# Layer 1 of the last two graphs regrouped, and unread TensorE products at both ends, in a two-layer graph-attention kernel

## The chip, the cores and the metric

The kernel runs on one core of a Trainium2 chip. The metric is the device time of one execution in microseconds (us). The core has five engines, each with an instruction queue of its own that is worked off in order: TensorE (PE in the profile, with its weight loads as PEld), VectorE (DVE), ScalarE (ACT), GpSimd (POOL) and SyncE (SP). DMA transfers are issued from POOL's and SP's queues.

## The reference: what is computed

The input x has 32 graphs of 512 nodes with 512 features, and all graphs share one 512 x 512 adjacency with about four neighbours to a node. Everything is float32. Both layers are added to x behind a layer norm and a relu (cut to its core):

```python
h = max(layernorm(x), 0)                              # layer 0: attention, 8 heads of 64
q, k, v = h @ Wq + bq, h @ Wk + bk, h @ Wv + bv
attn = softmax(q k^T / 8 + (1 - adj) * -1e9)
x = x + (attn @ v) @ Wo + bo
h = max(layernorm(x), 0)                              # layer 1: additive attention
g = h @ W
e = leaky_relu(g @ a1 [:, None] + g @ a2 [None, :], 0.2) * adj
x = x + elu(softmax(e) @ g + beta * g)
```

In layer 1 an edge that is absent has the score 0, not minus infinity, so every node also takes part in the sum of all nodes.

## The kernel before, in words

**Tiles.** A graph is four tiles of 128 nodes. The prediction numbers the token tiles of the second stage n = 4b + t with b the stage (0 to 33) and t the tile. The weights stay in SBUF. The neighbours of a tile's nodes are listed as edges; 128 edges make a group, and a tile has NG = 4 groups. Rows of keys, values and the layer-1 state are stored in DRAM tables (`tab`, for the last two stages `th`) and gathered back edge by edge by an indirect DMA from POOL, one for each group.

**Stages.** `stage_a(b)` makes q, k and v of graph b and stores them. `stage_b(b)` does layer 0 of graph b and, LAG = 2 graphs behind, layer 1 of graph b - 2. For b = 32 and 33 there is no layer 0 left (`s is None`): these two stages, n = 128 to 135, are layer 1 of the last two graphs, 30 and 31.

**One layer-1 tile** has these steps: four gathers (L946), the edge weights z (L1127 to L1134: sum of two scores, leaky relu on DVE, exponent on ACT, minus 1 on DVE), the weights spread to a one-hot matrix `wv` (L1140, DVE), the edge sums on PE (L987, four groups), a product that adds the denominators when there is no layer 0 (line 42 from `layer1`), the denominators on DVE (L1162 to L1164), the node's own row relu(norm(x1)) on ACT (L756) and its addition on DVE (L1170), four transposes on PE (L737), the addition of the column sums `cs` on ACT in four instructions (L1181), the product with W on PE (line 42 from `dense`, four blocks, eight records in the trace), two evictions on ACT (L1190, L1191), two elu steps on DVE (L1195, L1196) and a keep, the indirect DMA that writes the tile out (L767, POOL).

**What layer 1 needs of a whole graph.** The column sums `cs` and, in the last two graphs, s1: `spread_s1` transposes it on PE (L1100), writes it as one row to DRAM and reads it back to all partitions (SP, L1103 and L1108), and DVE picks the entries of each edge (L1112, L1113). A gather needs all four tiles of the graph stored (L1067).

**What sets the order.** Nothing is scheduled by hand. Each step is recorded with `op(engine, us, key, ...)`, with a cost and a due time `key`; S = 20 is the due-time distance of two tiles. `Plan.order` walks through time with these costs and picks, engine by engine, the ready operation with the lowest key. Its buffers are rings: `kv` (5 buffers of 128 x 2 x 1552, two to a tile), `oT` and `gT` (1 each, the transposed tiles), `w` (4), `z` (4), `wv` (2), six PSUM buffers `D` and one, `X`. A buffer is free when its last reader is done. The order found is fixed in the program; changing a key or a ring moves instructions of every queue.

**Start.** `setup` fills constants on DVE and POOL; x of graph 0 is loaded first, then the adjacency and the weights in pieces from SP (L775, L377, L645). The first PE work is `turned_state`'s transposes of the normed tiles, then `edges`' product for the node ranks (its input from L421) and the products with Wq, Wk and Wv.

Of the kernel before, what the change touches and what calls it, by code (L numbers as in the profile page):

```python
# [218 lines left out]
def kernel(  # L219
# [49 lines left out]
    def ring(n, shape, name):  # L269
# [52 lines left out]
    oh = OH.rearrange("p (g r) -> p g r", r=G)  # L322

    C_ = {n: buf(None, n) for n in (
        "wq", "wk", "wv", "wo", "w1", "rows", "c_row", "wa", "OH", "nzE", "idx", "qidx", "fin",
# [3 lines left out]
    def setup():  # L329
        nc.gpsimd.iota(OH.bitcast(I32), pattern=[[1, D]], base=1, channel_multiplier=0)  # L330
        nc.gpsimd.iota(idx[:, 0, 0:1], pattern=[[1, 1]], base=0, channel_multiplier=1)
        make_identity(nc, ident)
        nc.gpsimd.memset(mhalf, -0.5)
        nc.vector.memset(rings["qe"][-1], 0.0)
        nc.vector.memset(one32, 1.0 / G)
        for b in rings["hx"]:
            nc.vector.memset(b[:, D:], 0.0)
        for b in rings["q"]:
            nc.vector.memset(b[:, D:], 0.0)
        for b in rings["v"]:  # L340
# [343 lines left out]

    KD = 110.0

    def dot_rows():
# [47 lines left out]
    def turned(p, src):  # L735
        for c in range(C):
            nc.tensor.transpose(p[:, ts(c, P)], src[:, ts(c, P)], ident)  # L737
# [32 lines left out]
    def turned_state(b, t, key, mv):  # L770
        xb = buf("x", f"x{b}_{t}")
        if b:
            op("POOL", 1.3, key - 2.0 * S, lambda: fetch(xb.ap, b, t), r=[C_["perm"]], w=[xb], dma=P * D * 4)
        else:
            op("SP", 0.1, -90.0 + 0.01 * t, lambda: nc.sync.dma_start(xb.ap, x[0, ts(t, P), :]), w=[xb], dma=P * D * 4)  # L775
        norm(key - 1.3 * S, xb, mv, t, f"a{b}_{t}")
        op("ACT", 0.8, key - 0.9 * S, lambda: relu(xb.ap, xb.ap, mv.ap, t), r=[(mv, t)], w=[xb])
        pt, hT = buf("D", "pt"), buf("hT", f"hT{b}_{t}")
        kt = key + ((0.48, -0.51)[t % 2] if b else -0.51) * S
        o = op("PE", 0.45, kt, lambda: turned(pt.ap, xb.ap), r=[xb], w=[pt])  # L780
        plan.reserve(o, hT)
        op("ACT", 0.6, kt, lambda: nc.scalar.copy(hT.ap.rearrange("p c q -> p (c q)"), pt.ap), r=[pt], w=[hT])  # L782
        return hT
# [150 lines left out]
    def stage_b(b):  # L934
# [16 lines left out]
        for t in range(T):  # L951
            kb = base(T * b + t)
            slots = [buf("kv", f"kv{b}_{t}_{i}") for i in range(2)]
            held = [{n: buf(None, n) for n in ("K", "V", "H")} for _ in range(2)]
            of = {KO: "KVH", VO: "VH", HO: "H"}
            for g in range(NG):
                for tab, c0, c1 in st[b]["tab"]:
                    op("POOL", 1.3, kb - 0.85 * S + 0.1 * g, lambda sl=slots[g // 2], g=g, t=t, tab=tab, c0=c0, c1=c1: gather(
                        sl.ap[:, g % 2, c0:c1], tab, t, g),
                       r=[tab, C_["idx"]],  # L960
                       w=[(slots[g // 2], (g % 2, c0)), *((held[g // 2][n], (g % 2, "row")) for n in of[c0])],
                       dma=P * (c1 - c0) * 4)
# [18 lines left out]
        if s is not None:  # L981
            self_sums(b, base(T * b + 6))

    def edge_sums(out, lhs, slots, c0, n):

        for g in range(NG):
            nc.tensor.matmul(out(g), lhs(g), slots[g // 2].ap[:, g % 2, c0 : c0 + n], start=True, stop=True)  # L987

# [3 lines left out]
    def layer0(b, t, kb, slots, held, qs, weights):  # L992
# [126 lines left out]
    def edge_weights(b, t, kb, slots, held, qs):  # L1119

        s = st[b]
        k1 = kb + 0.6 * S
        z, wvb = buf("z", f"z{b}_{t}"), buf("wv", f"wv{b}_{t}")
        for i in range(2):
            def add(i=i):
                s1 = s["s1e"].ap[:, t, 2 * i : 2 * i + 2] if qs is None else qs[i].ap[:, :, D]
                nc.vector.tensor_tensor(z.ap[:, 2 * i : 2 * i + 2], s1, slots[i].ap[:, :, HO], op=ALU.add)  # L1127

# [7 lines left out]
        if b + LAG < B:  # L1136
            for i in range(2):
                op("DVE", 0.1, k1, lambda i=i: nc.vector.tensor_copy(
                    slots[i].ap[:, :, HO], z.ap[:, 2 * i : 2 * i + 2]), r=[z, (slots[i], "use")], w=[(held[i]["H"], "z")])
        op("DVE", 0.35, k1, lambda: nc.vector.tensor_tensor(  # L1140
# [4 lines left out]
    def layer1(b, t, kb, slots, held, wvb, pv):  # L1145
        s = st[b]
        px, g = buf("D", f"pg{b}_{t}"), buf("w", f"g{b}_{t}")
        o = op("PE", 1.02, kb + S, lambda: edge_sums(
            lambda i: px.ap[ts(i, G), :], lambda i: wvb.ap[:, ts(i, G)], slots, HO + 1, D),
               r=[*((x, "use") for x in slots), *((h["H"], "rows") for h in held), wvb], w=[px], form=4)  # L1150
        plan.reserve(o, g)
        k = kb + S
        x1, dn = s["x1"][t], s["dn"]
        op("ACT", 0.8, k, lambda: relu(g.ap, x1.ap, s["mv1"].ap, t), r=[x1, (s["mv1"], t)], w=[g])

        if pv is None:
            pd = buf("D", f"pn{b}_{t}")
            op("PE", 0.2, kb + S, lambda: product(nc, pd.ap[:, 0:1], wvb.ap, one32[:, 0:1]), r=[wvb], w=[pd])

# [24 lines left out]

        op("ACT", 1.5, k + 0.485 * S, add_all, r=[pt, s["cs"]], w=[gT])
        oo = op("PE", 3.43, k + 0.88 * S, lambda: dense(py.ap, gT.ap, w1), r=[gT, C_["w1"]], w=[py])
        plan.reserve(oo, y)
# [9 lines left out]

        op("ACT", 1.36, k + 1.05 * S, halves, r=[(dn, t)], w=[py, y])
        op("DVE", 1.45, k + 1.05 * S, elu, r=[py, x1], w=[y])
        op("POOL", 1.3, k + 1.2 * S, lambda: keep(y.ap, b, t), r=[y, C_["perm"]], dma=P * D * 4)  # L1200

# [247 lines left out]
```

## Time and profile before

| | us |
|---|---|
| median of 3 runs | 2736.29 (2734.39 to 2737.78) |
| profiled execution | 2723.47 |
| its span, first to last instruction | 2721.6 |
| PE busy | 2648.3 (97%) |
| DVE busy | 2049.9 (75%) |
| ACT busy | 1934.4 (71%) |
| POOL busy | 1831.2 (67%) |
| last W product on PE ends | 2711.4 |

The page is of one execution. A line of a timeline gives the start and the length in us, engine, source line, operation, output and input names with their shapes, a count, and in brackets the idle time of the engine just before and what ended it ("<-DVE w L1038": DVE's write of w at line 1038). "issue" is idle time for which the profile shows no other engine. A stretch's line gives its length and each engine's busy time with the number of its instructions, then the granted clock, the DMA share and GB/s. A product of float32 128 x 128 with 128 x 512 shows as two records; at the full clock records follow each other at 0.43 us, at half the clock at 0.85 us.

### The profile page before, as it was taken

The numbers are of one execution on the slowest core, as the hardware profiler recorded it, in microseconds if no ns is written. First come the engines' busy times: TensorE is split into PE (matmuls) and PEld (weight loads), VectorE is DVE, ScalarE is ACT, GpSimd is POOL, SyncE is SP. The second block draws the span as 40 slices with busy tenths as digits, with TensorE's granted clock in tenths as the row PEclk, the third lists the DMA queues.
The fourth block names the chain that finished last, engine by engine and source line by source line (L and its number), as shares of the span: only waits on it lengthen the run. The fifth ranks groups of instructions, "written<-read, shape, count | busy, mean of one in ns | idle before, by whom it ended". The sixth has DMA issues, their size and how long they took to land.

```text
span 2721.6 us, 39762 instructions
## 1 busy us (share of the span) xinstructions
PE 2648.3 (97%) x10220; PEld 1213.2 (45%) x10220; DVE 2049.9 (75%) x5200; ACT 1934.4 (71%) x6215; POOL 1831.2 (67%) x1710
## 2 busy tenths in 40 slices
PE   8999999999999999999999999999999999999886
PEld 4444444444444444444444444444444444444332
DVE  7768777777777777777777777777777777777663
ACT  1557777687877777777777777777777777777763
POOL 2776766666766766766766776676676676675763
PEclk9999999999999999999999999999999999999988
DMA  5988998888988988988988988988888888888863
GB/s 180 252 290 320 307 307 291 297 294 305 311 296 289 321 292 296 314 297 288 316 298 292 326 291 290 321 289 303 312 296 292 305 309 303 297 310 286 303 211 117
DMA packets 237457, 790.08 MB, mean 290 GB/s; under 512 B 34667, under 2 KB 34675, under 8 KB 237222
## 3 DMA queue, kind: packets, MB, share of 16 engines
q0 software_dynamic: 156736, 644.99, 70.3%
q1 hardware_dynamic: 80486, 142.48, 14.0%
q8 instruction: 83, 1.36, 0.2%
q14 instruction: 152, 1.25, 0.1%
HBM read 617.88 MB, written 169.46 MB: 289 GB/s over the span
## 4 chain that ended last, share of the span: by engine, by line
PE 88%; DMA 3%; issue 3%; DVE 2%; ACT 2%; POOL 2%; POOLq 0%; SPq 0%; DVEq 0%; ACTq 0%
PE pd L42 46%; PE pd L858 26%; PE pd L737 6%; PE pd L987 4%; PE px L987 4%; DMA qe<-qtab,qidx 1%; ACT kv L1014 1%; PE pd L918 1%; DMA kv<-tkv,idx 1%; PE pd L1081 1%; POOL kv L946 1%; POOL qe L968 0%; POOL x L762 0%; DMA x<-in_x_dram,perm 0%; DVE s L1003 0%
## 5 line engine op out<-in xcount | busy, mean ns | idle before, releaser
L1014 ACT ACTIVATE kv<-kv 128x64 f32<-128x64 f32 x4096 | 1011.8, 335 | 5.2
L968 POOL DMA_INDIRECT qe<-qtab,qidx x512 | 556.0, 1086 | 223.0 <-issue 114.0
L946 POOL DMA_INDIRECT kv<-tab,idx x480 | 508.2, 1059 | 164.6 <-issue 113.6
L42 PE MATMUL pd<-wo,oT 128*128 128x512 f32 x1032 | 468.6, 597 | 2.5 <-ACT oT L1051 2.4
L42 PE MATMUL pd<-w,gT 128*128 128x512 f32 x1024 | 466.1, 598 | 3.6 <-ACT gT L1181 3.6
L42 PE MATMUL pd<-wq,hT 128*128 128x512 f32 x1024 | 465.0, 597 | 2.2 <-ACT hT L782 2.2
L762 POOL DMA_INDIRECT x<-in_x_dram,perm x252 | 359.5, 1426 | 85.1 <-issue 50.3
L1000 DVE TENSOR_TENSOR qe<-qe,kv 128x1024 f32<-128x1024 f32 x256 | 312.1, 1220 | 44.4 <-DMA qe<-qtab,qidx 35.6
L1003 DVE TENSOR_REDUCE s<-qe 128x16 f32<-128x1024 f32 x256 | 310.5, 1214 | 0.1
L42 PEld LDWEIGHTS pd<-w,gT 128*128 128x128 f32 x1024 | 195.7, 192 | 249.5 <-issue 234.0
L42 PEld LDWEIGHTS pd<-wo,oT 128*128 128x128 f32 x1032 | 196.3, 192 | 245.0 <-issue 222.0
L42 PEld LDWEIGHTS pd<-wq,hT 128*128 128x128 f32 x1024 | 195.4, 192 | 245.6 <-issue 241.7
L749 POOL TENSOR_TENSOR mv<-mv,mhalf 128x1 f32<-128x1 f32 x256 | 171.4, 670 | 177.5 <-DVE mv L746 156.7
L767 POOL DMA_INDIRECT out_dram<-w,perm x128 | 157.3, 1229 | 149.8 <-DVE w L1196 105.7
L858 PE MATMUL pd<-wk,hT 128*128 128x512 f32 x496 | 239.7, 607 | 3.7 <-ACT hT L782 3.4
L858 PE MATMUL pd<-wt,S 128*128 128x512 f32 x496 | 238.5, 603 | 4.5 <-DVE k L866 4.1
L858 PE MATMUL pd<-wv,S 128*128 128x512 f32 x496 | 233.6, 593 | 3.1 <-DVE v L866 1.8
L1190 ACT ACTIVATE w<-pd,dn 128x512 f32<-128x512 f32 x128 | 87.6, 684 | 185.8 <-PE pd L42 185.5
L1061 DVE CUSTOM_DVE_ANT_0 w<-hx,wa_r 128x512 f32<-128x512 f32 x256 | 175.1, 684 | 11.3 <-ACT hx L756 10.5
L1053 DVE TENSOR_TENSOR x<-pd,x 128x512 f32<-128x512 f32 x128 | 87.9, 687 | 121.8 <-PE pd L42 110.1
L744 DVE BATCH_NORM_STATS2 st<-x 128x6 f32<-128x512 f32 x256 | 176.3, 689 | 3.8 <-DMA x<-in_x_dram 1.0
L737 PE MATMUL pd<-ident,w 128*128 128x128 f32 x1152 | 154.3, 276 | 21.7 <-DVE w L1038 11.2
(204 smaller groups left out, 3504.7 us busy)
## 6 DMA issues: line engine op xcount, KB each, us to landing
qtab<-q SPq DMA_DIRECT2D x124, 258.0 KB
tab<-hx SPq DMA_DIRECT2D x120, 260.0 KB
tab<-v SPq DMA_DIRECT2D x120, 260.0 KB
tab<-k SPq DMA_DIRECT2D x120, 256.0 KB
qe<-qtab,qidx POOLq DMA_INDIRECT x512, 7.8
kv<-tab,idx POOLq DMA_INDIRECT x480, 8.0
x<-in_x_dram,perm POOLq DMA_INDIRECT x252, 8.0
th<-hx SPq DMA_DIRECT2D x8, 260.0 KB
```

What stands on the lines that cost most here:

```text
L42: nc.tensor.matmul(out, lhsT, rhs, start=start, stop=stop)
L737: nc.tensor.transpose(p[:, ts(c, P)], src[:, ts(c, P)], ident)
L744: nc.vector.bn_stats(s6.ap, src.ap)
L762: nc.gpsimd.indirect_dma_start(dst, None, rows, bass.IndirectOffsetOnAxis(ap=perm[:, t : t + 1], axis=0), **lim)
L858: nc.tensor.matmul(p.ap, lhs()[:, c, :], rhs[:, c, :], start=first and c == 0, stop=c == K2 - 1, skip_group_check=True)
L946: nc.gpsimd.indirect_dma_start(dst, None, tab.ap, bass.IndirectOffsetOnAxis(ap=idx[:, t, g : g + 1], axis=0), bounds_check=N + DUMMY - 1, ...
L968: op("POOL", 1.3, kb - 0.84 * S + 0.1 * g, lambda q=qs[g // 2], g=g, t=t: nc.gpsimd.indirect_dma_start(q.ap[:, g % 2, :], None, s["qtab"]. ...
L987: nc.tensor.matmul(out(g), lhs(g), slots[g // 2].ap[:, g % 2, c0 : c0 + n], start=True, stop=True)
L1000: nc.vector.tensor_tensor(qe.ap[:, :, 0:D], qe.ap[:, :, 0:D], sl.ap[:, :, KO : KO + D], op=ALU.mult)
L1003: nc.vector.tensor_reduce(sb.ap, qe.ap[:, :, 0:D].rearrange("p n (h f) -> p n h f", f=HD), axis=AX.X, op=ALU.add)
L1014: nc.scalar.activation(p[:, h, 0:HD], p[:, h, 0:HD], AF.Copy, scale=p[:, h, HD : HD + 1])
L1061: nc.vector.tensor_tensor_reduce(scr.ap, hx.ap[:, 1 : D + 1], row, 1.0, 0.0, op0=ALU.mult, op1=ALU.add, accum_out=dst)
```

## The change

Layer 1 of the last two stages (b + LAG >= B in `layer1`, `s is None` in `stage_b`) is regrouped, and some products are added whose result nobody reads.

- **Rows in one buffer.** A tile of the last two stages takes one `kv` buffer and not two; its four rows of 520 lie one after the other in it. `row` and `weights_of` give the addresses of both layouts.
- **Sums ahead of products.** The due times of a layer-1 tile in the last two stages are moved: weights at 0.2 S after its base and not 0.6 S, edge sums at 0.5 S and not 1.0 S, while transposes, W product and evictions keep near the old ones. So the recorded order puts the edge sums of a tile ahead of the W product of the tile before.
- **One add.** The four additions of `cs` on ACT become one instruction on DVE, and the transposed tile lies in `gT` and `oT` in turn.
- **Unread products.** `run_on` records a number of 128 x 128 by 128 x 512 products into a PSUM buffer that is written again before it is read. At the start three of them, on a constant block that DVE sets to 1 (`first`), ahead of the first transposes. Near the end three each at n = 124 and 125, which wait for the tile's first gather, and one each for n = 123 to 127, behind the edge sums of layer 0. In PE's order the two threes come to lie just ahead of Wo of n = 122 and between the two transposes of n = 123.

PE's order is the same as before from the first transposes until n = 122, and so is that of the other queues up to there, DVE's new memset aside.

```diff
@@ setup
+        nc.vector.memset(first[:, 0:D], 1.0)
@@
+    GL, ZL = 0.5, 0.2
...
+    def run_on(key, n, bank, src, us=0.86, behind=()):
+
+        def prod():
+            for _ in range(n):
+                product(nc, bank.ap, src[:, 0:P], src[:, 0:D])
+
+        op("PE", us * n, key, prod, r=behind, w=[bank])
@@ turned_state
+        if b == 0 and t == 0:
+            run_on(kt, 3, pt, first, 1.7)
@@ stage_b
-            slots = [buf("kv", f"kv{b}_{t}_{i}") for i in range(2)]
+            slots = [buf("kv", f"kv{b}_{t}_{i}") for i in range(2 if s is not None else 1)]
+            slots += slots[len(slots) - 1 :] * (2 - len(slots))
@@
+    def row(slots, g, c0, n):
+
+        if slots[0] is slots[1]:
+            return slots[0].ap.rearrange("p a b -> p (a b)")[:, g * HW_ + c0 - HO : g * HW_ + c0 - HO + n]
+        return slots[g // 2].ap[:, g % 2, c0 : c0 + n]
@@ layer0
+        if T * b + t > T * (B - 1) - 2:
+            run_on(k + 0.01, 1, pt, wq[:, 0, :], behind=[px])
@@ edge_weights
-        k1 = kb + 0.6 * S
+        k1 = kb + (0.6 if b + LAG < B else ZL) * S
@@ layer1
-        o = op("PE", 1.02, kb + S, lambda: edge_sums(
+        last = b + LAG >= B
+        k = kb + (GL if last else 1.0) * S
+        kt, kw, ke = (0.6 - GL, 1.7 - GL, 1.75 - GL) if last else (0.485, 0.88, 1.05)
+        if b + LAG == B - 1 and t < 2:
+            run_on(k - 0.2, 3, px, wq[:, 0, :], behind=[(slots[0], (0, KO))])
+        o = op("PE", 1.02, k, lambda: edge_sums(
...
-        pt, gT, py, y = buf("D", "pt"), buf("gT", f"gT{b}_{t}"), buf("D", "py"), buf("w", f"y{b}_{t}")
-        oo = op("PE", 0.45, k + 0.485 * S, lambda: turned(pt.ap, g.ap), r=[g], w=[pt])
+        pt, gT, py, y = buf("D", "pt"), buf("oT" if last and t % 2 else "gT", f"gT{b}_{t}"), buf("D", "py"), buf("w", f"y{b}_{t}")
+        oo = op("PE", 0.45, k + kt * S, lambda: turned(pt.ap, g.ap), r=[g], w=[pt])
...
+        def add_at_once():
+            nc.vector.tensor_tensor(
+                gT.ap, pt.ap.rearrange("p (c q) -> p c q", c=C), s["cs"].ap.unsqueeze(2).to_broadcast([P, C, P]), op=ALU.add)
+
+        if last:
+            op("DVE", 0.72, k + kt * S, add_at_once, r=[pt, s["cs"]], w=[gT])
+        else:
+            op("ACT", 1.5, k + kt * S, add_all, r=[pt, s["cs"]], w=[gT])
+        oo = op("PE", 3.43, k + kw * S, lambda: dense(py.ap, gT.ap, w1), r=[gT, C_["w1"]], w=[py])
```

More of the change, by code (lines that the diff above doesn't have):

```diff
@@ L322 @@
     oh = OH.rearrange("p (g r) -> p g r", r=G)
+    first = rings["kv"][0][:, 0, :]
     C_ = {n: buf(None, n) for n in (
@@ L957, in stage_b @@
                 for tab, c0, c1 in st[b]["tab"]:
-                    op("POOL", 1.3, kb - 0.85 * S + 0.1 * g, lambda sl=slots[g // 2], g=g, t=t, tab=tab, c0=c0, c1=c1: gather(
-                        sl.ap[:, g % 2, c0:c1], tab, t, g),
+                    op("POOL", 1.3, kb - 0.85 * S + 0.1 * g, lambda slots=slots, g=g, t=t, tab=tab, c0=c0, c1=c1: gather(
+                        row(slots, g, c0, c1 - c0), tab, t, g),
                        r=[tab, C_["idx"]],
-                       w=[(slots[g // 2], (g % 2, c0)), *((held[g // 2][n], (g % 2, "row")) for n in of[c0])],
+                       w=[(slots[g // 2], (g, c0)), *((held[g // 2][n], (g % 2, "row")) for n in of[c0])],
                        dma=P * (c1 - c0) * 4)
@@ L982, in stage_b, with weights_of @@
             self_sums(b, base(T * b + 6))
+    def row(slots, g, c0, n):
+        if slots[0] is slots[1]:
+            return slots[0].ap.rearrange("p a b -> p (a b)")[:, g * HW_ + c0 - HO : g * HW_ + c0 - HO + n]
+        return slots[g // 2].ap[:, g % 2, c0 : c0 + n]
+    def weights_of(slots, i):
+        if slots[0] is slots[1]:
+            flat = slots[0].ap.rearrange("p a b -> p (a b)")[:, 0 : NG * HW_]
+            return flat.rearrange("p (g c) -> p g c", g=NG)[:, 2 * i : 2 * i + 2, 0]
+        return slots[i].ap[:, :, HO]
     def edge_sums(out, lhs, slots, c0, n):
         for g in range(NG):
-            nc.tensor.matmul(out(g), lhs(g), slots[g // 2].ap[:, g % 2, c0 : c0 + n], start=True, stop=True)
+            nc.tensor.matmul(out(g), lhs(g), row(slots, g, c0, n), start=True, stop=True)
     def use(slots, held, names):
@@ L1126, in add @@
                 s1 = s["s1e"].ap[:, t, 2 * i : 2 * i + 2] if qs is None else qs[i].ap[:, :, D]
-                nc.vector.tensor_tensor(z.ap[:, 2 * i : 2 * i + 2], s1, slots[i].ap[:, :, HO], op=ALU.add)
+                nc.vector.tensor_tensor(z.ap[:, 2 * i : 2 * i + 2], s1, weights_of(slots, i), op=ALU.add)
             op("DVE", 0.2, k1, add, r=[*([s["s1e"]] if qs is None else [(qs[i], "use"), qs[i].s1]),
@@ L1138, in edge_weights @@
                 op("DVE", 0.1, k1, lambda i=i: nc.vector.tensor_copy(
-                    slots[i].ap[:, :, HO], z.ap[:, 2 * i : 2 * i + 2]), r=[z, (slots[i], "use")], w=[(held[i]["H"], "z")])
+                    weights_of(slots, i), z.ap[:, 2 * i : 2 * i + 2]), r=[z, (slots[i], "use")], w=[(held[i]["H"], "z")])
         op("DVE", 0.35, k1, lambda: nc.vector.tensor_tensor(
@@ L1151, in layer1 @@
         plan.reserve(o, g)
-        k = kb + S
         x1, dn = s["x1"][t], s["dn"]
@@ L1157, in layer1 @@
             pd = buf("D", f"pn{b}_{t}")
-            op("PE", 0.2, kb + S, lambda: product(nc, pd.ap[:, 0:1], wvb.ap, one32[:, 0:1]), r=[wvb], w=[pd])
+            op("PE", 0.2, k, lambda: product(nc, pd.ap[:, 0:1], wvb.ap, one32[:, 0:1]), r=[wvb], w=[pd])
         def den():
@@ L1183, in add_all @@
                 )
-        op("ACT", 1.5, k + 0.485 * S, add_all, r=[pt, s["cs"]], w=[gT])
-        oo = op("PE", 3.43, k + 0.88 * S, lambda: dense(py.ap, gT.ap, w1), r=[gT, C_["w1"]], w=[py])
+        def add_at_once():
[6 more added lines that the diff above has]
+        oo = op("PE", 3.43, k + kw * S, lambda: dense(py.ap, gT.ap, w1), r=[gT, C_["w1"]], w=[py])
         plan.reserve(oo, y)
@@ L1196, in elu @@
             nc.vector.tensor_tensor(y.ap, y.ap, py.ap, op=ALU.add)
-        op("ACT", 1.36, k + 1.05 * S, halves, r=[(dn, t)], w=[py, y])
-        op("DVE", 1.45, k + 1.05 * S, elu, r=[py, x1], w=[y])
-        op("POOL", 1.3, k + 1.2 * S, lambda: keep(y.ap, b, t), r=[y, C_["perm"]], dma=P * D * 4)
+        op("ACT", 1.36, k + ke * S, halves, r=[(dn, t)], w=[py, y])
+        op("DVE", 1.45, k + ke * S, elu, r=[py, x1], w=[y])
+        op("POOL", 1.3, k + (ke + 0.15) * S, lambda: keep(y.ap, b, t), r=[y, C_["perm"]], dma=P * D * 4)
     def judge():
```

## The prediction

> **What bounds the kernel now.** I read the 40 slices first: in which stretch does TensorE (PE) stand, and in which is it slow?
>
> ```profile
> PE   8999999999999999999999999999999999999886
> PEld 4444444444444444444444444444444444444332
> DVE  7768777777777777777777777777777777777663
> ACT  1557777687877777777777777777777777777763
> POOL 2776766666766766766766776676676676675763
> PEclk9999999999999999999999999999999999999988
> ```
>
> PE is at nine tenths everywhere but in the first slice and the last two or three, and there its granted clock falls too. In between PE is the bound. The change leaves PE's order between its two ends as it was, so nothing is to be won or lost there. The stretches by time show how large the end is:
>
> ```profile
> core 0: us, PE busy (x) PEld busy (x) DVE busy (x) ACT busy (x) POOL busy (x), PEclk, DMA share, GB/s
> 2430.00:2540.00 110.00, 109.76 (x409) 49.56 (x411) 83.82 (x207) 80.61 (x266) 70.48 (x66) 1.00 0.86 302
> 2540.00:2642.60 102.60, 80.62 (x363) 36.43 (x360) 69.48 (x189) 75.17 (x248) 72.02 (x63) 0.90 0.80 259
> 2642.60:2711.50 68.90, 55.04 (x198) 22.15 (x196) 29.53 (x98) 26.35 (x65) 32.56 (x33) 0.93 0.46 136
> ```
>
> Up to 2540 PE is full. In the second stretch (the last six token tiles that still have layer 0; I number tiles n, so these are n = 122 to 127) it stands 22.0 us, in the third (after Wo of n = 127, when only the eight layer-1 tiles 128 to 135 and the W product of 127 are left) 13.9 us, and no other engine is full there. So the third stretch is a chain. PE's timeline shows which:
>
> ```profile
> 2680.22 1.07 PE L987 MATMUL pd<-kv,wv 128*32 128x512 f32 x8
> 2682.32 0.66 PE L737 MATMUL pd<-ident,w 128*128 128x128 f32 x4 [0.72 <-DVE w L1170]
> 2683.49 3.70 PE L42 MATMUL pd<-w,gT 128*128 128x512 f32 x8 [0.52 <-ACT gT L1181]
> 2687.12 1.06 PE L987 MATMUL pd<-kv,wv 128*32 128x512 f32 x8
> 2691.11 0.65 PE L737 MATMUL pd<-ident,w 128*128 128x128 f32 x4 [2.61 <-DVE w L1170]
> ```
>
> One tile is edge sums, then DVE's own-row step (L1170), transposes, ACT's four adds (L1181), then the W product: each waits for the one before, and PE has nothing of another tile between. Why nothing? GpSimd's (POOL's) timeline:
>
> ```profile
> 2671.14 1.00 POOL L946 DMA_INDIRECT kv<-th,idx  x1 [3.35 <-PE pd L42]
> 2672.44 1.00 POOL L946 DMA_INDIRECT kv<-th,idx  x1 [0.30 <-issue]
> 2673.75 1.00 POOL L946 DMA_INDIRECT kv<-th,idx  x1 [0.30 <-issue]
> 2675.05 1.03 POOL L767 DMA_INDIRECT out_dram<-w,perm  x1 [0.30 <-issue]
> ```
>
> The gathers wait for PE to free a `kv` buffer (two per tile, five in all), though POOL itself needs only 1.31 us a transfer: four gathers and a keep are 6.5 us against a pitch of 8.3 us from 2649.42 to 2707.68 (seven tiles).
>
> Last, the clock at the stands:
>
> ```profile
> 2636.06 1.31 PE L737 MATMUL pd<-ident,w 128*128 128x128 f32 x8 [1.16 <-DVE w L1038]
> 2637.39 5.40 PE L42 MATMUL pd<-wo,oT 128*128 128x512 f32 x8
> ```
>
> A W or Wo product takes 3.70 us; this one takes 5.40, because four of its eight records ran at half speed (0.85 us instead of 0.43). In the third stretch three of nine products do so: 5.1 us.
>
> **Start: three unread products, 1.71 us each at half clock.** They run from the end of the new DVE memset of `first` (1.02 + half of the 0.92 us of the memset twice its width = 1.5 us) to 1.6 + 5.1 = 6.7 us; PE's first transpose starts at 6.67. The memset is ahead of DVE's other setup, which ends at 2.6; DVE then stands 0.98 us until x lands at 3.59, so it costs nothing; without that cover 0.46. What can be won: from 10.87 (DVE's L421) the dense products run at half clock until 16.11, where the record pitch turns from 0.85 to 0.43; six records x 0.43 = 2.6 us. By the Trainium skill (TensorE: Matmul & The Clock Gate, Part 1) the clock opens after a busy window of about 3.4 us and closes after an idle one, and the window runs free; by that rule the three products open it before 8.4, the transposes that follow leave no window wholly idle, and the sum is -2.6. The rows are harder: at 2637.39 the clock closed though the window before held 1.31 us of transposes, the end of the edge sums and 0.38 us more, some 65% busy. (In this trace the turns at 16.11, 2572.8, 2668.3 and 2695.6 all lie on one 3.41 us grid, so the windows can be laid over the rows.) Between 6.7 and 10.87 there are three sets of transposes, 0.6 us each at full clock, so a window there is about half busy and closes again. I take 0; bounds -2.6 and +0.3 (transposes pushed by the tail of the third product).
>
> **n = 122 to 127, 102.6 us.** Eleven unread products come in: three each between the transposes and Wo of 122 and between the two transposes of 123 (they wait only for a first gather of 124 and 125, which POOL issued at 2550 and 2564), and one behind each edge sum of 123 to 127. At full clock 0.86 us each: 9.5 us, at half 18.8. The first triple meets a stand of 0.23 us, so 2.4 us delay Wo of 122; but next come stands of 2.64 and 4.44 us, set by DVE and by the edge weights of 124, and they swallow both triples. The singles meet stands of 1.16 to 1.26 us. By the skill's table (same page, Why this matters for your kernels) only idle gaps over about 3 us are to be avoided; by it these fillers gain nothing and can only cost. The row at 2637.39 speaks for them: a stand of 1.16 us with transposes cost 1.7 us.
>
> More comes from the order that moves with them. On ACT the exponent of 124's weights stood behind the two W evictions of 123 (2580.49; the exponent at 2581.63) and now stands behind 123's four adds, ahead of sixteen head scalings. On POOL two query gathers of 125 now come before two kv gathers of 126, a keep, the norm's power and a fetch. I followed the four queues with the durations of the trace: edge sums of 124 end 2.8 us earlier than 2586.9, those of 125 4 us, of 126 only 1.2 (DVE: exponent behind evictions again), of 127 about 3. Two Wo products of four keep the clock. Wo of 127 then ends near 2638.5 instead of 2642.6: **-4.1 us**, bounds -8 and +4 (products uncovered, clock closing anyway).
>
> POOL's wait for the edge sums of 127 (it holds 131's first gather) stands, as before, ahead of the fetch of 127's x and so of table 31. Moved past: the power of 126 stands now behind eight gathers (10.5 us) and not four. It waited for DVE until 2631.37; eight gathers from about 2618.5 end at 2629, so nothing; if POOL is late there, up to 1.6 us for DVE's queue behind it. On SP only graph 30's read-back of s1 moves one store ahead: nothing, SP stands for most of this stretch.
>
> **n = 128 to 135, 68.9 us.** These are 13.9 stand + 5.1 half clock + 49.9 work. Now four rows of 520 lie in one buffer (2080 of 3104 columns), so five tiles can be gathered ahead; PE does transposes of n, denominators and edge sums of n+1 (1.33 us), then the product of n. Under these lie the add in one DVE instruction and its wait: nearest row the division L1038 (PSUM source, broadcast operand), 0.68 us; with 0.25 of hand-over 0.93, less than 1.33. The add leaves ACT (4 instructions, 1.14 us) and puts 8 x 0.68 = 5.4 us on DVE, which has 39 us free in this stretch: nothing; without the cover 0.4 us a tile. Its two target buffers alternate, so it doesn't wait for the product before.
>
> What is late next:
> - Graph 31's edge weights need s1 of all its rows: transposed on PE, written and read back by SP (2656.01 to about 2661), picked by DVE in two steps. In DVE's new order the pick stands behind the add of 131. Product of 130 ends 22 us after Wo of 127, transposes and add 1.4, pick 1.3, the elu of 130 that stands ahead of the weights 1.4, weights and exponent 1.6: PE waits **5.2** us for the sums of 132. Such a stand closes the clock: **+1.7**.
> - Last tile: no other sums cover its add, +1.0.
> - POOL: after the fetch of 127 moves 4 us up, table 31's last rows land near 2650 (store at 2650.59 - 4, landing 3.6 us as the gathers' own). Then 16 gathers and 3 keeps x 1.31 = 24.9, landing 3.6, weights 1.2: 2680. PE wants the last tile's sums near 2684. Hidden, by 4 us only. If a keep waits for its elu, the gathers behind it in POOL's queue wait as well.
>
> 49.9 + 5.2 + 1.7 + 1.0 = 57.8: **-11.1 us**, bounds -18 (neither the wait nor the clock) and -3 (a stand of 1 us left in each tile). The 10.2 us after the last product (eviction, elu, keep, its landing) stay.
>
> **Sum.** 0 - 4.1 - 11.1 = -15.2. The profiled execution was 2723.47 us (span 2721.6), so 2708.3; the median of the runs shown is 2736.29, 12.8 above it without the end being any different, so I take the same difference: **2721**.
>
> **Rivals.**
> - A, the above, 0.55: 2721.
> - B, DVE's queue takes over (0.20). In the new order the first weight steps of 128, 129 and 130 stand in DVE's queue ahead of 126's and 127's own steps, and each waits for a gather. A 0.9 us stand per tile remains (7), the rest as in A: -8, 2728. For it: DVE stood 20.8 us of the last 220 on such gathers. Against: four or eight gathers now have the whole of 126 to land.
> - C, all falls into place (0.12): clock opened at the start (-2.6), Wo of 127 4 us earlier still, half of the wait for s1 hidden: -24, 2712.
> - D, slower (0.05): the unread products between 2558 and 2640 lie uncovered at half clock. 11 x 1.71 = 18.8 us on PE's path instead of -4.1; with -11.1 after it +7.7, less some cover: 2742. It decides from the point at which more than 11 of the 18.8 us are uncovered; for it speaks the 0.23 us stand at the first triple, against it 8.5 us of stands before the edge sums of 124 and 125 that no product fills.
> - E, the change doesn't do what it says (0.08): the clock closes anyway, the products cost what the new order gains, and B's stands are 1.3 us: 2735.
>
> **Range and chances.** 2711 to 2731 leaves out D, E and the ends of B and C, 0.2. A measurement of this kernel can tell about 0.2% (5.5 us) from no change: faster below 2730.8 (A, C, most of B) 0.84, within 0.11, slower 0.05.
>
> **What would show it.** Right: PE stands under 8 us after Wo of 127, one of them about 5 us before the first sums of graph 31; pairs of edge sums and products without a wait for DVE's add; no gather waiting for PE there; a pitch near 6 us; Wo of 127 some 4 us earlier. At the start a pitch of 0.85 from 10.87 on. Wrong: the first full-speed record before 13 (start wins), the triples followed by a later edge sum of 124 (D), waits for DVE's L1170 successor in every tile (B), or POOL's keeps waiting in front of gathers.

## The result, and the profile after

The changed kernel takes 2721.65 us (median of 6 runs, 2717.14 to 2724.40); the kernel before took 2733.63 in the 6 runs that stand beside them. The ratio is 0.9957, 95% interval 0.9946 to 0.9968: 12 us less, where the prediction's sum was 15.2.

The profiled execution of the changed kernel took 2724.40 us, 0.9 us *more* than the profiled one of before. The two pages alone would say that the change did nothing, so the views have to be read by stretches. The slices of the page first:

```profile
PE   9999999999999999999999999999999999999986
...
PEclk9999999999999999999999999999999999999998
```

PE's last slices are fuller than before, and its granted clock drops only in the last one. The stretches by time, cut as before (Wo of n = 127 ends at 2650.2, the last W product at 2712.4):

```profile
core 0: us, PE busy (x) PEld busy (x) DVE busy (x) ACT busy (x) POOL busy (x), PEclk, DMA share, GB/s
2548.70:2650.20 101.50, 85.64 (x385) 37.33 (x381) 69.47 (x190) 76.05 (x249) 78.19 (x69) 0.95 0.86 277
2650.20:2712.50 62.30, 50.32 (x198) 21.93 (x198) 33.36 (x105) 17.41 (x32) 26.16 (x27) 0.89 0.40 120
```

The third stretch has gone from 68.9 to 62.3 us, but PE still stands 12.0 us in it. Its later tiles look as forecast. PE's timeline:

```profile
2691.76 0.60 PE L741 MATMUL pd<-ident,w 128*128 128x128 f32 x4
2692.19 0.28 PE L42 MATMUL pd<-one,wv 128*128 128x1 f32 x2
2692.40 1.07 PE L1015 MATMUL pd<-kv,wv 128*32 128x512 f32 x8
2693.41 3.70 PE L42 MATMUL pd<-w,gT 128*128 128x512 f32 x8
2696.95 0.60 PE L741 MATMUL pd<-ident,w 128*128 128x128 f32 x4
```

No line has a bracket: transposes of one tile, denominators and sums of the next, product of the first, without a wait. An undisturbed tile takes 5.19 us here, where it took 6.90 before (sums at 2680.22 to sums at 2687.12 in the prediction's lines); the 8.3 of the prediction is the mean from n = 128 to 135, and that mean is 7.4 now. GpSimd's waits in this stretch (in total, times, longest) show that no gather waits for PE any more; 0.30 us each is its issue:

```profile
POOL out_dram L779 <- DVE w L1238: 23.1, 5, 5.5
...
POOL kv L960 <- issue: 4.3, 14, 0.3
```

PE's 12 us lie ahead of that, where graph 31 takes over from graph 30:

```profile
2667.25 1.07 PE L1015 MATMUL pd<-kv,wv 128*32 128x512 f32 x8
2669.70 3.70 PE L42 MATMUL pd<-w,gT 128*128 128x512 f32 x8 [1.38 <-DVE gT L1221]
2676.18 1.12 PE L741 MATMUL pd<-ident,w 128*128 128x128 f32 x4 [2.78 <-issue]
2684.34 0.58 PE L42 MATMUL pd<-one,wv 128*128 128x1 f32 x2 [7.03 <-DVE wv L1170]
```

DVE's timeline for the same time has two waits whose end the profile can put down to no instruction ("remote"): its own-row step of n = 131 and the addition behind it.

```profile
2675.38 0.75 DVE L1205 SCALAR_TENSOR_TENSOR w<-w,dn,pd 128x512 f32<-128x512 f32 x1 [3.96 <-remote]
...
2679.65 0.69 DVE L1221 TENSOR_TENSOR oT<-pd,cs 128x512 f32<-128x512 f32 x1 [3.44 <-remote]
```

The own-row step needs the sums that PE ran from 2667.25 to 2668.3, yet it starts at 2675.38. A signal is the update by which an engine tells the others that an instruction has ended, and the trace has a table of their times. In it the four signals of these sums arrive at 2671.0, 2671.7, 2673.9 and 2675.3. That of the W product which ended at 2673.4 arrives at 2679.57, that of the transposes behind it at 2679.62. DVE's own-row step, ACT's eviction and DVE's addition start 0.02 to 0.1 us after the last signal that each needs. PE's signals are late, by up to 7 us. In the same table fifteen signals before 900 us are 1.3 us or more late; the profile of before has none ahead of its last product. The experiments show that this is no part of the change: of 14 profiles of 13 kernels five have late PE signals (this one and the four of e5 to e8), with only 1612 to 1693 of some 1930 PE signals recorded; the nine others have none there, and all but a few records. From Wo product 40 to 118, where every kernel has the same order, it takes 1577.0 to 1577.1 us without them and 1578.4 to 1579.4 with them. So times are compared below by the ratio to runs of the kernel before beside them, and stretches among profiles of one kind.

### The profile page after: what moved, and what is told of

Same layout as the page of the kernel before. It is cut to its first block, busy times and chain, and to the rows that moved or that the text cites. A ratio compares the mean times of both kernels' runs of the same rounds, so it can differ in the third digit from the quotient of the medians.

```text
span 2722.6 us, 39798 instructions
## 1 busy us (share of the span) xinstructions
PE 2657.9 (98%) x10248; PEld 1216.0 (45%) x10248; DVE 2054.8 (75%) x5209; ACT 1931.4 (71%) x6183; POOL 1818.6 (67%) x1710
## 4 chain that ended last, share of the span: by engine, by line
PE 88%; issue 3%; POOL 3%; DVE 2%; DMA 2%; ACT 1%; another core or an unknown queue 0%; POOLq 0%; SPq 0%; DVEq 0%; ACTq 0%
PE pd L42 46%; PE pd L872 26%; PE pd L741 6%; PE pd L1015 4%; PE px L1015 4%; POOL kv L960 1%; PE pd L932 1%; PE pd L1111 1%; DMA qe<-qtab,qidx 1%; POOL qe L983 1%; DMA x<-in_x_dram,perm 1%; POOL x L774 0%; ACT kv L1042 0%; DMA kv<-tkv,idx 0%
## 5 line engine op out<-in xcount | busy, mean ns | idle before, releaser
L983 POOL DMA_INDIRECT qe<-qtab,qidx x512 | 546.8, 1068 | 229.9 <-issue 123.2
L42 PE MATMUL pd<-w,gT 128*128 128x512 f32 x992 | 446.4, 593 | 1.4 <-DVE gT L1221 1.4
L774 POOL DMA_INDIRECT x<-in_x_dram,perm x252 | 352.0, 1397 | 85.8 <-issue 46.4
L42 PEld LDWEIGHTS pd<-w,gT 128*128 128x128 f32 x992 | 188.1, 190 | 239.7 <-issue 231.2
L741 PEld LDWEIGHTS pd<-ident,w 128*128 128x128 f32 x1152 | 133.5, 142 | 82.7 <-issue 46.8
```

The costliest lines, as they stand in the source:

```text
L42: nc.tensor.matmul(out, lhsT, rhs, start=start, stop=stop)
L774: nc.gpsimd.indirect_dma_start(dst, None, rows, bass.IndirectOffsetOnAxis(ap=perm[:, t : t + 1], axis=0), **lim)
L983: op("POOL", 1.3, kb - 0.84 * S + 0.1 * g, lambda q=qs[g // 2], g=g, t=t: nc.gpsimd.indirect_dma_start(q.ap[:, g % 2, :], None, s["qtab"]. ...
```

## The experiments

Each stretch is from a kernel's one profile. "Last stretch" is from the start of Wo of n = 127 to the end of the last W product; what follows it is 10.23 or 10.24 us in every kernel.

| kernel | ratio to before (95%) | Wo 121 to Wo 127 | last stretch | late PE signals |
|---|---|---|---|---|
| before | 1 | 91.1 | 74.0 | no |
| changed | 0.9957 (0.9946-0.9968) | 91.5 | 65.9 | yes |
| e1 no start products | 0.9937 (0.9924-0.9951) | 89.8 | 58.8 | no |
| e2 no end products | 0.9951 (0.9937-0.9964) | 92.4 | 59.8 | no |
| e3 regrouping alone | 0.9961 (0.9948-0.9975) | 93.3 | 58.4 | no |
| e4 unread products alone | 1.0002 (0.9994-1.0010) | 88.3 | 74.4 | no |
| e5 changed, again | 0.9948 (0.9935-0.9960) | 94.0 | 66.5 | yes |
| e6 old due times | 1.0027 (1.0018-1.0036) | 91.9 | 82.8 | yes |
| e7 two buffers a tile | 0.9950 (0.9936-0.9963) | 93.4 | 63.9 | yes |
| e8 sums of 132 later | 0.9950 (0.9932-0.9967) | 92.1 | 65.2 | yes |
| e9 four additions | 0.9952 (0.9939-0.9965) | 90.8 | 58.3 | no |
| e10 one buffer alone | 0.9983 (0.9976-0.9991) | 90.9 | 67.4 | no |
| e11 pick ahead | 0.9948 (0.9935-0.9961) | 90.0 | 58.3 | no |
| e12 both | 0.9941 (0.9927-0.9954) | 90.4 | 58.1 | no |

The kernel before took 2725.51, 2741.88 and 2721.79 us (medians) beside e1 to e4, e5 to e8 and e9 to e12: the absolute times in the expectations hold for another level, and what is compared is their distance from the changed kernel or from before.

**e1, no start products.**

```diff
-        nc.vector.memset(first[:, 0:D], 1.0)
-        if b == 0 and t == 0:
-            run_on(kt, 3, pt, first, 1.7)
```

> The changed kernel without the three unread products at the start and without the memset that feeds them; all else stays. Theory (the prediction's): they neither open the clock for good nor delay anything, since the changed kernel's clock opened for one window of 3.4 us and closed again from 9.4 to 16.2 us: the time stays that of the changed kernel, 2721.7 within 2, and the first dense products run at half speed until about 16 us as they do in the kernel before. Rival: the products help later in the start and this kernel is 2.6 us or more slower, 2724.3 or above. Second rival: they cost, since the first Wo product came 1.0 us later in the changed kernel's profile than in the profile of before: then about 2720.7.

Nothing is lost without them: 0.9937 stands beside the changed kernel's 0.9957 and 0.9948, and the intervals overlap. The profile is the most useful of all, since it has the changed kernel's order at the end without late signals. Its stretch after Wo of n = 127, and PE's timeline between the graphs:

```profile
2643.60:2698.80 55.20, 49.71 (x200) 21.82 (x198) 33.33 (x105) 17.27 (x32) 26.34 (x27) 0.94 0.46 137
```

```profile
2660.89 1.08 PE L1012 MATMUL pd<-kv,wv 128*32 128x512 f32 x8
2661.89 3.70 PE L42 MATMUL pd<-w,gT 128*128 128x512 f32 x8
2665.43 0.60 PE L740 MATMUL pd<-ident,w 128*128 128x128 f32 x4
2670.72 0.59 PE L42 MATMUL pd<-one,wv 128*128 128x1 f32 x2 [4.69 <-DVE wv L1167]
2671.24 1.93 PE L1012 MATMUL pd<-kv,wv 128*32 128x512 f32 x8
2673.10 5.14 PE L42 MATMUL pd<-w,oT 128*128 128x512 f32 x8
```

The first four lines are the operations that the changed kernel's fence showed: from sums to denominators it takes 9.8 us (2660.89 to 2670.72), where late signals made it 17.1 (2667.25 to 2684.34). These 7.3 us account for the difference of the two last stretches (7.1 us: 65.9 against 58.8). One long stand is left, for the weights of graph 31, and the trace has the clock at half from 2669.2 to 2676.0.

What the products do at the start is read from all profiles. PE's timeline of e2, which has them, ahead of that of the changed kernel's first profile, which has them too:

```profile
11.21 1.10 PE L42 MATMUL pd<-kv,x 128*128 128x512 f32 x2 [1.29 <-DVE kv L424]
12.14 3.60 PE L42 MATMUL pd<-wq,hT 128*128 128x512 f32 x8
```

```profile
11.61 2.05 PE L42 MATMUL pd<-kv,x 128*128 128x512 f32 x2 [2.02 <-DVE kv L424]
13.45 5.44 PE L42 MATMUL pd<-wq,hT 128*128 128x512 f32 x8
```

In the one the clock opened at 6.2 us and stayed open until 47.1; in the other it opened at 6.9, closed at 10.3 and opened again at 17.1 (9.4 and 16.2 in e1's expectation are 0.9 us too early). Of the eleven profiles with the products six are of the first kind (the next product begins at 15.4 to 15.8 us), five of the second (17.0 to 18.7); the three without have 17.8, 18.3 and 18.7. The gain is 2.7 us at best and nothing at worst. It goes with how full PE is in the windows of 3.41 us on whose grid the clock turns: from the opening on, PE's rows fill 43 to 54% of the windows after which the clock closed, and 49 to 69% of those after which it stayed open. At the first Wo product the six stand at 111.2 us on average, the five at 114.6, the three without at 113.9: 1.1 us on average over the eleven, less than the times can tell.

**e2, no end products; e3, neither; e4, unread products alone.** e2 leaves out the two threes and the five singles, e3 the start products as well. e4 keeps all of them and undoes the regrouping:

```diff
-            slots = [buf("kv", f"kv{b}_{t}_{i}") for i in range(2 if s is not None else 1)]
+            slots = [buf("kv", f"kv{b}_{t}_{i}") for i in range(2)]
-        k1 = kb + (0.6 if b + LAG < B else ZL) * S
+        k1 = kb + 0.6 * S
-        k = kb + (GL if last else 1.0) * S
-        kt, kw, ke = (0.6 - GL, 1.7 - GL, 1.75 - GL) if last else (0.485, 0.88, 1.05)
+        k = kb + 1.0 * S
+        kt, kw, ke = 0.485, 0.88, 1.05
-        if last:
+        if False:
             op("DVE", 0.72, k + kt * S, add_at_once, r=[pt, s["cs"]], w=[gT])
-        pt, gT, py, y = buf("D", "pt"), buf("oT" if last and t % 2 else "gT", f"gT{b}_{t}"), buf("D", "py"), buf("w", f"y{b}_{t}")
+        pt, gT, py, y = buf("D", "pt"), buf("gT", f"gT{b}_{t}"), buf("D", "py"), buf("w", f"y{b}_{t}")
```

> The changed kernel without the eleven unread products near the end (two threes and five singles); start and regrouping stay. Theory: the singles lie in stands and cost nothing, the first three cost 2.2 us of PE's path in the changed kernel's profile, and all together keep the clock at one or two Wo products (1.7 us each) and bring about the better order on ACT and POOL: without them 2723 to 2726, that is 1 to 4 us slower. Rival: they only cost, 9.5 us of PE work of which 2.2 or more lies on the path: without them 2719.5 or below. The order near n = 124 changes with them, so the stretch from Wo of n = 121 to Wo of n = 127 is to be read beside the time (91.5 us in the changed kernel's profile, 91.1 in that of before).

> The regrouping of layer 1 alone: no unread products at either end. Theory: the stretch from Wo of n = 127 to the end carries the gain (76.1 us in the changed kernel's profile, of which some 6 us were a late semaphore of PE; 84.2 in that of before), so this kernel has most of it: 2722 to 2726, with that stretch at 70 to 76 us. Rival: the gain comes from the unread products: then 2730 or above, with the stretch above 80 us.

> The unread products at both ends alone: rows of layer 1 in two buffers, due times, four adds on ACT and one transposed buffer as before. Theory: start nothing, the stretch from Wo of n = 121 to Wo of n = 127 within 4 us of that of before (91.1), the stretch after it as before (84.2): 2730 to 2734. Rival: unread products carry the gain: 2725 or below. Second rival: they lie uncovered on PE's path: 2736 or above.

The last stretch answers: 58.4 us with the regrouping alone, 74.4 with the unread products alone, 74.0 before. The regrouping takes all of the 15.6 us off it, and e4's time is that of before. The products at the end shorten only the stretch ahead, Wo 121 to Wo 127: by 3.5 us beside the regrouping (e1 against e3), by 2.8 without it (e4 against before). All profiles without late signals fit this: the regrouped kernels with these products have 89.8 to 90.9 us there, the two without them 92.4 and 93.3. In the times it doesn't show: e4's ratio is 1.0002 over 13 runs, its profiled execution (2720.53 us) was the fastest of them, and the intervals of e1, e2 and e3 overlap. So the 3 us are seen in profiles only, and e2's two cases, 1 to 4 us slower or 2 us faster, are not told apart by its time: its 0.9951 lies between the changed kernel's 0.9957 and 0.9948.

**e5, the changed kernel again.** No edit.

> The changed kernel as it is, once more, for its profile. Theory: its first profile was disturbed (signals of PE came up to 7 us after the end of the work that sends them, at 2668 to 2680 us and at a dozen places before 900 us, and records of signals are missing): an undisturbed one has 1577.0 us between Wo products 40 and 118 as all others have, and from Wo of n = 121 to the end 158.5 to 160.5 us (158.8 without the start products, 175.3 before). Rival: what stands at 2671 to 2684 belongs to the kernel: 165 us or more from Wo of n = 121 to the end, as in the first profile (167.7).

The theory fell in its first half: the signals were late again, and from Wo of n = 121 to the end it took 170.7 us. So it was no accident of one execution. But the rival, that these microseconds belong to the kernel, falls with e1 (158.8, the same order). They go with the chip or the set of runs: e5 to e8 ran on one chip and all have them, e1 to e4 and e9 to e12 ran on two others and have none. A profile of the kernel before with late signals is missing, so what they cost that kernel is known from the times alone.

**e6, old due times; e9, four additions; e10, one buffer alone.** e6 sets the due times back (the three lines of e4's diff), e9 only `if last:` to `if False:`, e10 does all of e4's diff but the first pair of lines, so that of the regrouping only the one buffer is left. By these lines the change moves a tile's transposes as well: from 1.485 S after its base to 0.6 S, right behind its sums, and not near the old place as "The change" says. The W product goes from 1.88 to 1.7 S, behind the next tile's sums (1.5 S).

> The changed kernel with one buffer for the four rows and with the one addition on DVE, but with the old due times for the last two stages: PE does transposes, W product, then the edge sums of the next tile, which stand ahead of its own-row step again. Theory: gathers no longer wait for PE, but each tile still is a chain of own-row step, transposes, addition and W product: of the 15 us that the stretch from the start of Wo of n = 127 to the last W product has lost in the regrouped kernels (74.0 to 58.8) 5 to 10 stay won: 64 to 69 us there. Rival: the buffer alone does it, 58 to 60 us; second rival: the order alone does it, 72 to 74 us.

> The changed kernel with the four additions on ACT in place of the one on DVE (targets still alternate, due times and buffers as changed). Theory: with the next tile's sums and denominators (1.3 us) between transposes and W product the addition is covered either way, ACT has room, so the stretch from Wo of n = 127 to the last W product stays within 2 us of the changed kernel on the same chip (66 us where signals of PE come late, 59 to 60 where they don't), and the ratio to the kernel before stays 0.994 to 0.996. Rival: the one addition is what makes the order work; four of them let the product wait about 0.5 us a tile: 4 us more, 0.996 to 0.9975.

> Of the regrouping only the one buffer for the four rows: old due times, four additions on ACT, one target; the unread products stay. Theory: more gathers ahead win nothing while each tile is a chain on PE (the kernel with two buffers and the new due times lost nothing against the changed one): 72 to 76 us from Wo of n = 127 to the last W product, ratio 0.998 to 1.001. Rival (the prediction's view): the gathers' wait for a free buffer sets the pitch of 8.3 us; without it 1 us a tile is won, 64 to 68 us, ratio 0.9955 to 0.998.

e6 met none of its three cases: it is slower than before. PE's timeline of e6 and DVE's for its first tile there, then one tile in PE's timeline of e10:

```profile
2695.49 0.66 PE L741 MATMUL pd<-ident,w 128*128 128x128 f32 x4 [0.71 <-DVE w L1205]
2697.86 3.70 PE L42 MATMUL pd<-w,gT 128*128 128x512 f32 x8 [1.71 <-DVE gT L1221]
...
2705.96 5.40 PE L42 MATMUL pd<-w,oT 128*128 128x512 f32 x8 [1.71 <-DVE oT L1221]
```

```profile
2695.74 0.68 DVE L1237 SCALAR_TENSOR_TENSOR w<-w,x 128x512 f32<-128x512 f32 x1
2696.52 0.69 DVE L1238 TENSOR_TENSOR w<-w,pd 128x512 f32<-128x512 f32 x1
2697.13 0.68 DVE L1221 TENSOR_TENSOR gT<-pd,cs 128x512 f32<-128x512 f32 x1
```

```profile
2679.01 0.66 PE L741 MATMUL pd<-ident,w 128*128 128x128 f32 x4 [0.72 <-DVE w L1205]
2680.18 3.70 PE L42 MATMUL pd<-w,gT 128*128 128x512 f32 x8 [0.52 <-ACT gT L1216]
```

In the old order both wait for the own-row step, but the W product waits up to 2.4 us for the one addition on DVE, and 0.5 for the four on ACT. The addition itself is not slow (0.68 us): in DVE's order the two elu steps of the tile before (L1237, L1238) stand ahead of it. The W products' waits from n = 128 on sum to 11.4 us in e6 and 3.4 in e10, and four products of e6 ran partly at half clock (6.75, 6.60, 5.40 and 5.40 us: 9.4 us lost; e10 lost 2.3 in one). 8.0 + 7.1 are 15.1 of the 15.4 us between 82.8 and 67.4; e6 was recorded with late signals, but in this stretch none is over 1.3 us late. So the one addition, with the place that it has in DVE's queue there, needs the order that covers it; a DVE order with the addition ahead of the elu steps was not tried. With the order, four additions do as well: e9 has 58.3 us, and its W products from n = 128 on wait 1.6 us for them in all, where e1's wait 0.8 for the one. That is not the additions alone, since other places of PE's order moved with them: s1's transpose comes 6.6 us after Wo of n = 127 and not 12.6, and the stand of 4.69 us is gone, with stands of 2.08 and 1.62 us behind it instead.

e10 shows the prediction's cause by itself. GpSimd's waits of the kernel before and of e10, after Wo of n = 127:

```profile
POOL kv L946 <- PE pd L42: 9.9, 5, 4.2
```

```profile
POOL kv L960 <- PE pd L42: 0.6, 2, 0.3
```

With one buffer a tile no gather waits for PE beyond 0.30 us, the mean pitch from n = 128 to 135 falls from 8.3 to 7.2 us and the last stretch from 74.0 to 67.4 (e4, the same kernel with two buffers, has 74.4). So my theory that this alone wins nothing is wrong, though the time hardly tells: 0.9983 is just outside the rival's range.

**e7, two buffers a tile.**

```diff
-            slots = [buf("kv", f"kv{b}_{t}_{i}") for i in range(2 if s is not None else 1)]
+            slots = [buf("kv", f"kv{b}_{t}_{i}") for i in range(2)]
```

> The changed kernel with two buffers of the five for each tile of the last two stages as before; due times, one addition and alternating targets stay changed. Theory: the gathers wait for PE's edge sums to free buffers again (13.3 us in that stretch before), and since four gathers and a keep take 6.6 us of POOL and 3.6 us more until they land, the sums of the next tile come late: 65 to 70 us from Wo of n = 127 to the last W product. Rival: the order is all and the buffers don't matter: 58 to 60 us.

Beside the changed kernel of its own set (e5) the rival is right; its 58 to 60 us was meant for a profile without late signals. Of the gathers' wait for PE little is left, since sums that come ahead of the product also free the buffers earlier:

```profile
POOL kv L960 <- PE pd L1015: 3.9, 2, 2.1
```

The last stretch is 63.9 us where e5 has 66.5, and the ratios are equal; how much of the 2.6 us is late signals can't be told. The two cures for one wait don't add: one buffer alone wins 6.6 us, order and buffer 15.2 to 15.7 (e1, e3, e9), and taking the buffer out again costs nothing that can be measured.

**e8, sums of 132 later; e11, pick ahead; e12, both.** Two ways at the one stand that is left, one diff each; e12 has both. e8 moves one due time, and e11's line gives the read-back of s1 a shorter transfer in the plan alone, which changes nothing but the order:

```diff
+        GL = 0.75 if b == B - 1 and t == 0 else 0.5
         k = kb + (GL if last else 1.0) * S
```

```diff
-           r=[row], w=[s1b], dma=P * N * 4)
+           r=[row], w=[s1b], dma=2048)
```

> The changed kernel with one due time moved: the edge sums of the first tile of graph 31 (n = 132), which wait for s1 of the whole graph, are due behind the W product of n = 131 instead of ahead of it. Theory: PE's stand of 4.7 us before these sums (seen without the start products) is filled by that product, which then also runs at the full clock (3.7 and not 5.1 us): 5 us less, 53 to 55 us from Wo of n = 127 to the last W product where e1 has 58.8. Rival: the wait only moves, to the addition that nothing covers then (1 us), to the sums of n = 133 or to gathers behind a later keep: 58 us or more.

> The changed kernel, in whose plan alone the read-back of s1 is given a shorter transfer, so that DVE's order has the pick of graph 31's entries ahead of the addition of n = 131 and not behind it (two denominators of 128 and 129 also move up on PE). Theory: in the profile without start products DVE stood 1.7 us just ahead of that addition while the row had been read back 5 us earlier; with the pick there PE's stand of 4.7 us before the sums of 132 shrinks by 1.3 to 2.5: stretch of 56 to 58 us from Wo of n = 127 to the last W product on a chip without late signals (64 to 66 with them), ratio 0.1% or less below the changed kernel's. Rival: the row lands later than the pick is due and DVE's queue waits behind it: no change or 1 to 2 us more.

> As the kernel before this one, and the sums of n = 132 due behind the W product of n = 131 as well. Theory: that product (3.7 us) takes the place of the stand and the pick is done in time: 53 to 55 us from Wo of n = 127 to the last W product on a chip without late signals, 4 to 6 us less than the changed kernel on the same chip, ratio 0.992 to 0.994. Rival: the uncovered addition of n = 131 and a later signal take it back: within 2 us of the changed kernel.

e8 ran with late signals, among them the one ahead of the very product that should fill the stand (it waited 4.93 us), and says little. e11's stand is 3.55 us and e12's product of n = 131 is in its place, at the full clock. PE's timeline of e12:

```profile
2666.90 3.70 PE L42 MATMUL pd<-w,oT 128*128 128x512 f32 x8 [0.78 <-DVE oT L1222]
2670.44 0.28 PE L42 MATMUL pd<-one,wv 128*128 128x1 f32 x2
2670.65 1.07 PE L1015 MATMUL pd<-kv,wv 128*32 128x512 f32 x8
2674.14 0.66 PE L741 MATMUL pd<-ident,w 128*128 128x128 f32 x4 [2.42 <-DVE w L1206]
...
2686.49 0.38 PE L42 MATMUL pd<-one,wv 128*128 128x1 f32 x2 [1.17 <-DVE wv L1170]
```

But the wait has moved, as the rival said: behind the sums of 132 PE has nothing but their own transposes (2.42 us), the weights of n = 135 come 1.17 us late, and PE's order around 128 and 129, which moved too, has 1.7 us of stands that the changed kernel's hasn't. 58.1 and 58.3 us are no gain over e1's 58.8. None of the versions beats the changed kernel beyond the intervals.

## Why the prediction came out right, step by step

**The sum.** Forecast -15.2 us, measured -12.0 (ratio 0.9957) and, in e5, 0.9948. In the profiles without late signals the end alone, from Wo of n = 121, is 16.6 us shorter (175.3 to 158.8 in e1). The mechanism and its place are right, and e1, without late signals, shows most of the signs that the prediction set: PE stands 5.5 us after Wo of n = 127 (under 8; 12.0 in the changed kernel's own profile), 4.69 of it before the first sums of graph 31, and no gather waits for PE. That the median fell on 2721 is partly luck. I took the profiled execution to be 12.8 us below the median for no reason tied to the kernel and moved this over. The profile of before has no late signals; the runs beside e5 to e8, which have them, lie higher (2741.88), and with them the changed kernel loses 7 us between the graphs that it doesn't lose without.

**n = 128 to 135, forecast -11.1.** In e1 from the end of Wo of n = 127 to the last W product: 68.6 to 55.1, so -13.5. The stand for graph 31's weights was 4.69 (forecast 5.2), that of the last tile 0.79 (1.0), and the clock cost 2.6 (1.7): 1.4 in the product, the rest in denominators and sums. What was mis-sized is "49.9 work". I took off only the three half-speed products, 5.1 us; PE's busy time there fell from 54.7 to 49.6 although e1 loses 2.6 to the clock itself, so the work is 47.0 and the old order's loss was 7.7. The other 2.6 are no clock. A tile of the old order keeps PE busy for 5.66 us (6.90 less waits of 0.72 and 0.52), one of the new order for 5.19: with no wait behind them the transposes take 0.44 us until the next operation begins and not 0.66, the denominators 0.21 and not 0.38. The keep of n = 128 did hold the gathers of graph 31 in POOL's queue (4.55 us, until 2651.96 in e1), without cost: these weights waited for the pick of s1 anyway, which DVE began at 2666.68.

**Why the pitch was 8.3.** "The gathers wait for PE to free a buffer" is a true cause (e10: 1.1 us a tile), but half of the answer: without that wait each tile was still a chain of own-row step and addition, 1.2 us of waits. In e1, with order and buffer, the mean is 6.4 us, the stand of 4.69 included. The order removes both waits, the buffer one.

**n = 122 to 127, forecast -4.1.** In e1 Wo of n = 127 ends 3.1 us earlier, counted from Wo of n = 121 (96.51 to 93.45). The first three cost 2.2 (forecast 2.4). Sums of 124 came 2.6 us earlier (2.8), of 125 3.6 (4), of 127 1.6 (3), and those of 126 0.8 *later* (1.2 earlier). The prediction had those of 126 held only by ACT's exponent; what held them is DVE's new order and the norm's power of 125. PE's, DVE's and POOL's timelines of e1, then DVE's of before, in this order:

```profile
2621.94 2.03 PE L1012 MATMUL pd<-kv,wv 128*32 128x512 f32 x8 [4.47 <-DVE wv L1167]
```

```profile
2618.66 0.16 DVE L762 SCALAR_TENSOR_TENSOR mv<-mv 128x1 f32<-128x1 f32 x1 [1.52 <-POOL mv L760]
2618.74 1.21 DVE L1028 TENSOR_REDUCE s<-qe 128x16 f32<-128x1024 f32 x1
2619.87 0.68 DVE L1234 SCALAR_TENSOR_TENSOR w<-w,x 128x512 f32<-128x512 f32 x1
2620.66 0.69 DVE L1235 TENSOR_TENSOR w<-w,pd 128x512 f32<-128x512 f32 x1
2621.60 0.28 DVE L1167 TENSOR_TENSOR wv<-OH,z 128x128 f32<-128x128 f32 x1
```

```profile
2615.99 2.04 POOL L980 DMA_INDIRECT qe<-qtab,qidx  x1 [0.30 <-issue]
2618.04 0.59 POOL L760 TENSOR_TENSOR mv<-mv,mhalf 128x1 f32<-128x1 f32 x1
```

```profile
2616.63 0.16 DVE L751 SCALAR_TENSOR_TENSOR mv<-mv 128x1 f32<-128x1 f32 x1 [0.74 <-POOL mv L749]
2616.84 0.28 DVE L1140 TENSOR_TENSOR wv<-OH,z 128x128 f32<-128x128 f32 x1
```

DVE stood 1.52 us for the power of 125 (0.74 before), which POOL had behind a query gather of 2.04 us (1.00 in its place before). Behind that step a reduction and two elu steps now stand in DVE's queue ahead of the weights of 126, so that these come 2.94 us after it; before they came 0.21 us after it. This term the prediction did not have. The one that it had, the power of 126 behind eight gathers ("so nothing; if POOL is late there, up to 1.6 us for DVE's queue behind it"), took the end of its range: DVE stood 1.77 us for it at 2635.87, but PE then stands only 0.62 us ahead of the next transposes (2638.61). The changed kernel itself, with late signals, ended Wo of n = 127 only 1.3 us earlier (95.2) in its first profile, and 1.2 us later in e5 (97.7).

**Start, forecast 0 with -2.6 as bound.** Both occur: -2.7 in six of eleven profiles, about 0 in five. I argued from one border (65% busy closed the clock) as if it held elsewhere and the rows lay still in the windows. Neither is so: here twelve windows of 58 to 66% stayed open, and the rows move against the windows. By the Trainium skill (TensorE: Matmul & The Clock Gate, Part 1) the free-running window makes the number of slow products vary from run to run by its phase at the start; these fourteen profiles agree. The phase alone doesn't decide: the clock opened at 5.6 us in e5 and in e8, and closed again in e8 only, where the first product behind the transposes stood 1.91 us for its input and not 1.47. It should have been half of the bound.

**Rivals.** B (DVE's queue, 0.9 us in each tile) didn't occur: from n = 132 on no transposes and no product waits but the last. Nor did D: the unread products near the end ran at full speed in the changed kernel (2.74 us for three, 1.12 for one), though in e1 one of the singles took 1.90. E's half that the unread products give back what they gain is nearer to the times (e4: 1.0002) than my -4.1, which the profiles support and the times can't tell.

## What to carry to other kernels

Where each tile at a kernel's end is a chain, put the next tile's first step ahead of this tile's last in the engine's order; that alone also frees buffers earlier, so test it before adding buffers. Price an operation that moves to another engine (four additions on ACT, one on DVE) by what stands ahead of it in that engine's queue, in both orders: covered it cost nothing, uncovered and behind two elu steps 15 us (8 of waits, 7 of clock). Before a difference of two profiles is explained, compare a stretch in which both kernels have the same order: here Wo of n = 121 began 8.7 us later in the profile after than in that of before, and hid a shorter end.

## What was not expected of the hardware

PE's signals to the other engines can arrive up to 7 us after the end of the work, several in a row, while PE itself goes on at full speed; DVE's and ACT's don't (none over 0.5 us ahead of the last transfers). It came in all four profiles of the set e5 to e8, which ran on one chip, and in none of the two sets on two other chips; the chip of the first pair isn't known. Within that pair the changed kernel has late signals and the kernel before has none. It cost the changed kernel 7 us at 2668 to 2680; the kernel before took 2741.88 us beside the set with it and 2725.51 and 2721.79 beside the sets without. It goes with missing records of signals, and not of PE's alone: of some 4130 of DVE's the five profiles have 3192 to 3301, though DVE's are not late. Whether the recording causes it or only suffers from the same thing stays open: no time here comes without a record of the run. Why it strikes between graphs 30 and 31, where gathers follow each other without a gap, stays open too.
